# Two 7x7 grouped convolutions: from multiply-adds on VectorE to row-banded matmuls on TensorE

## The chip, the cores and the metric

The kernel runs on one core of a Trainium2 chip. The metric is the device time of one execution in microseconds (us). The core has a matrix engine (TensorE, PE in the profile, with PEld for its weight loads), a vector engine (VectorE, DVE), an activation engine (ScalarE, ACT), GpSimd (POOL) and a queue engine (SyncE, SP). Sixteen DMA engines move data between device memory (DRAM) and the on-chip memory SBUF, whose 128 partitions are the rows of every tile. Matmuls write into PSUM, which has eight banks of 128 partitions x 512 floats.

## The reference, cut to what matters

All numbers are 32-bit floats. x has 2 images of 256 channels, 64 x 64 pixels.

```
# layer 0: global attention over the 4096 pixels, 8 heads of 32 channels, then a 1x1 fuse
attn = softmax(q k^T);  fuse = attn v
x = conv1x1(concat[x, fuse], Wf) * m + x * (1 - m)          # m: mask, resized bilinearly
# layer 1: channel gate, attention in 8x8 windows (4 heads of 64), then the spatial gate:
x = x * sigmoid(mlp(x));  x = x + window_attention(x) @ out_w
x = x.reshape(b, 4, 64, h, w).transpose(0, 2, 1, 3, 4).reshape(b, 256, h, w)   # channel shuffle
y = conv7x7(x, sa_w1, pad 3, groups 64)      # 4 input channels -> 1 output channel, 64 groups
y = relu(bn1(y + sa_b1))
y = conv7x7(y, sa_w2, pad 3, groups 64)      # 1 input channel -> 4 output channels, 64 groups
return x * sigmoid(bn2(y + sa_b2))
```

Group g of the first convolution reads the four channels g, 64 + g, 128 + g and 192 + g of the unshuffled x, and makes one channel; the second makes the four gates of the same group out of it.

## The kernel before, in words

First q, k and v of layer 0 are computed for both images, 16 chunks of 512 pixels, and stored in DRAM. Then one function, `pipeline`, runs everything else in an order written out by hand (`tc.manual_schedule()`): each engine executes its instructions in the order in which the Python code emits them, and waits on semaphores where data are not ready. Two copies of it are built, `arm("a")` and `arm("b")`, with and without a shift of the softmax by a row maximum; a flag computed on the chip picks one. The profile is of arm a.

The main loop goes over 1024 slots (b, c, g, m): image, chunk of 512 query pixels, half of the heads, block of 128 key pixels. A slot has `scores(i + 1)` (four matmuls with 32 rows of weights each, side by side in the array, L398; two exponentials on ScalarE, L406) and `products(i)` (four matmuls for attention times v, L418, and four for the row sums, L421, each 32 columns wide, side by side). The scores use PSUM tiles of two banks, of which there are three (`psum2`); convolutions and stages take theirs from the same three. `load_piece` asks for the k and v of eight slots, two pieces ahead, on SP's queue.

When a chunk's 64 slots are over, `stage(b, c)` does the rest of layer 0 and layer 1's gate and window attention for those 8 image rows. It is a generator: each fourth slot runs it to its next `yield`, 14 steps in all, so that its matmuls stand between those of the slots. Its last step writes the 8 rows into two zero-bordered images in SBUF, `xp[0]` and `xp[1]` (L632), and queues the convolutions whose rows are complete.

The convolutions before are on VectorE. `conv1(b, r0, r1)` makes up to 16 rows: for each of 49 taps and of the two channel halves one instruction, `z = xp[shifted] * w + z` (`tap`, L650 for the first and L652 for the rest), then a matmul with a 0/1 matrix that adds partition halves (`fold`, L669) and a ReLU with the batch norm as scale and bias into `yp` (L670). `conv2` does 49 taps per channel half on `yp`; then tanh and a rescaling on ScalarE make the sigmoid (L433, L434), VectorE multiplies by x (L695), and two stores on GpSimd's queue write the result (L699). `run_convs(2.2)` emits taps of a planned 2.2 us after each slot, so VectorE's other work stands between taps. After the last slot a loop emits what is left: the last stage and the convolutions that remain.

Of the kernel before, what the change touches and what calls it, by code (L numbers as in the profile page):

```python
# [34 lines left out]
HP = H + 2 * PAD  # L35
# [7 lines left out]
def conv_seq_kernel(ctx: ExitStack, tc: tile.TileContext, a, out):  # L43
    nc = tc.nc
    const = ctx.enter_context(tc.tile_pool(name="const", bufs=1))
    dram = ctx.enter_context(tc.tile_pool(name="dram", bufs=1, space=bass.MemoryType.DRAM))
# [17 lines left out]
    def load(name, shape, src, eng, pool=const):  # L64
        t = pool.tile(shape, F32, name=name)
        eng.dma_start(t, src)
        return t

    xp = []
    for kc in range(KC):  # L70
        t = const.tile([P, HP, HP], F32, name=f"xp_{kc}")
        nc.gpsimd.memset(t, 0.0)
        xp.append(t)
    yp = const.tile([P, HP, HP], F32, name="yp")
    nc.gpsimd.memset(yp, 0.0)
# [12 lines left out]
    }  # L88
    k_s, v_s = (
# [119 lines left out]
    sw1 = load("sa_w1", [P, 2, KS * KS], a["sa_w1"], nc.scalar)  # L209
    sw2 = load("sa_w2", [P, 2, KS * KS], a["sa_w2"], nc.scalar)  # L210
# [3 lines left out]
    def batch_norm(name, vec, n):  # L214
        t = const.tile([P, 5, n], F32, name=name)
        if vec.shape[0] == P:
            nc.scalar.dma_start(t, vec)
        else:
            for h in range(2):
                nc.scalar.dma_start(t[64 * h : 64 * h + 64], vec)  # L220
        g, beta, mean, var, cbias = (t[:, i, :] for i in range(5))
        sc = const.tile([P, n], F32, name=name + "_sc")
        sh = const.tile([P, n], F32, name=name + "_sh")
        nc.vector.tensor_scalar_add(sc, var, EPS)
        nc.scalar.activation(sc, sc, AF.Sqrt)
        nc.vector.reciprocal(sc, sc)
        nc.vector.tensor_mul(sc, sc, g)
        nc.vector.tensor_sub(sh, cbias, mean)
        nc.vector.tensor_mul(sh, sh, sc)
        nc.vector.tensor_add(sh, sh, beta)  # L230
        return sc, sh

    sc1, sh1 = batch_norm("bn1", a["bn1"], 1)
    sc2, sh2 = batch_norm("bn2", a["bn2"], 2)

    for t in (sc2, sh2, cb2):
        nc.vector.tensor_scalar_mul(t, t, 0.5)


    fold = const.tile([P, P], F32, name="fold")  # L240
    for i in range(2):
        for j in range(2):
            nc.vector.tensor_copy(
                fold[64 * i : 64 * i + 64, 64 * j : 64 * j + 64],
                ident[64 * i : 64 * i + 64, 64 * i : 64 * i + 64],
            )

# [17 lines left out]
    taps = [(dy, dx) for dy in range(KS) for dx in range(KS)]  # L265


    def conv_rows(b):
        if b + 1 < B:
            steps = {1: (13, 10), 3: (29, 26), 5: (45, 42), 7: (64, 64)}  # L270
        else:
            steps = {1: (13, 10), 3: (29, 26), 5: (45, 42), 6: (53, 50), 7: (64, 64)}
        r1 = r2 = 0
        parts = {}
        for c, (e1, e2) in steps.items():
            parts[c] = (split(r1, e1), split(r2, e2))
            r1, r2 = e1, e2
        return parts

    def split(r0, r1):  # L280
        n = -(-(r1 - r0) // 16)
        cuts = [r0 + (r1 - r0) * i // n for i in range(n + 1)]
        return list(zip(cuts, cuts[1:]))

# [5 lines left out]
    def pipeline(arm, shifted, pools):  # L290
        kvp, qp, ep, fp, xpool, gp, wp, cp = pools
# [139 lines left out]

        def sigmoid(t, z, bias, scale):
            nc.scalar.activation(t, z, AF.Tanh, bias=bias, scale=scale)  # L433
            nc.scalar.activation(t, t, AF.Copy, bias=0.5, scale=0.5)  # L434
# [34 lines left out]
        def stage(b, c):  # L469
# [159 lines left out]
            yield  # L629
            for oc in range(KC):  # L630
                r = PAD + WS * c
                nc.vector.tensor_add(  # L632
                    xp[oc][:, r : r + WS, PAD : PAD + W].rearrange("p r (w c) -> p w r c", c=WS),
                    y[:, oc, :].rearrange("p (w r c) -> p w r c", w=NW, r=WS),
                    u[:, oc, :].rearrange("p (w r c) -> p w r c", w=NW, r=WS),
                )
            if c in parts[b]:
                for r0, r1 in parts[b][c][0]:
                    convs.append(conv1(b, r0, r1))
                for r0, r1 in parts[b][c][1]:  # L640
                    convs.append(conv2(b, r0, r1))

        parts = [conv_rows(b) for b in range(B)]

        def tap(dst, src, wgt, r0, r1, i, first):
            dy, dx = taps[i]
            view = src[:, dy + r0 : dy + r1, dx : dx + W]
            wi = wgt[:, i : i + 1]
            if first:
                nc.vector.tensor_scalar_mul(dst, view, wi)  # L650
            else:
                nc.vector.scalar_tensor_tensor(dst, view, wi, dst, ALU.mult, ALU.add)  # L652
# [3 lines left out]
        def conv1(b, r0, r1):  # L656
            n = r1 - r0
            z = cp.tile([P, 16, W], F32, tag="acc", name=f"acc{arm}_{b}_{r0}")[:, 0:n, :]
            for kc in range(KC):
                for i in range(len(taps)):  # L660
                    tap(z, xp[kc], sw1[:, kc, :], r0, r1, i, kc == 0 and i == 0)
                    yield n * W / 960 + 0.16
            yield 0
            yield 0
            s = psum2(f"fold{arm}_{b}_{r0}")
            sr = s.rearrange("p a (r w) -> p (a r) w", w=W)
            for q0 in range(0, n, 8):
                q1 = min(q0 + 8, n)
                nc.tensor.matmul(sr[:, q0:q1, :], fold, z[:, q0:q1, :], start=True, stop=True)  # L669
            nc.scalar.activation(  # L670
                yp[:, PAD + r0 : PAD + r1, PAD : PAD + W],
                sr[:, 0:n, :],
                AF.Relu,
                bias=sh1,
                scale=sc1,
            )
            yield 0


        dst = [out[b].rearrange("(j k h) r w -> h k j r w", k=2, h=2) for b in range(B)]  # L680

        def conv2(b, r0, r1):
            n = r1 - r0
            for kc in range(KC):
                z = cp.tile([P, 16, W], F32, tag="z", name=f"z{arm}_{b}_{r0}_{kc}", bufs=2)
                z = z[:, 0:n, :]
                for i in range(len(taps)):
                    tap(z, yp, sw2[:, kc, :], r0, r1, i, i == 0)
                    yield n * W / 960 + 0.16

                def gate(z=z, kc=kc):
                    sigmoid(z, z, sh2[:, kc : kc + 1], sc2[:, kc : kc + 1])

                def finish(z=z, kc=kc):
                    nc.vector.tensor_mul(  # L695
                        z, z, xp[kc][:, PAD + r0 : PAD + r1, PAD : PAD + W]
                    )
                    for h in range(2):
                        nc.gpsimd.dma_start(  # L699
                            dst[b][h, kc, :, r0:r1, :], z[64 * h : 64 * h + 64]  # L700
                        )

                at(2, gate)
                at(4, finish)

        def run_convs(budget):
            while convs and budget > 0:
                cost = next(convs[0], None)
                if cost is None:
                    convs.popleft()  # L710
                elif cost == 0:
                    return
                else:
                    budget -= cost
# [21 lines left out]
        for i, (b, c, g, m) in enumerate(slots):  # L736
            now[0] = i
            if m % PB == 0:
                load_piece(i // PB + 2)
            if g == KC - 1 and m == 0:  # L740
                nxt = (b, c + 1) if c + 1 < NCHUNK else (b + 1, 0)
                if nxt[0] < B:
                    load_q(*nxt)
            if i + 1 < len(slots):
                scores(i + 1)
            products(i)
            if g == KC - 1 and m == NMB - 1:
                at(4, lambda b=b, c=c: stages.append(stage(b, c)))
                if c == NCHUNK - 1 and b + 1 < B:
                    at(32, lambda b=b: load_mask(b + 1))  # L750
            run_later()
            if i % 4 == 0:
                run_stages()
            run_convs(2.2)
        while stages or convs or later:
            now[0] += 1
            run_later()
            run_stages()
            run_convs(2.2)

    def arm(name, shifted):
        with (
# [7 lines left out]
            tc.tile_pool(name=f"c{name}", bufs=1) as cp,  # L770
            tc.manual_schedule(),
        ):
            pipeline(name, shifted, (kvp, qp, ep, fp, xpool, gp, wp, cp))
# [71 lines left out]
```

## Time and profile before

| what | value |
|---|---|
| median of 3 runs | 4376.79 us (4374.94 to 4377.25) |
| the profiled execution's own time | 4377.27 us |
| its span, first to last instruction | 4375.5 us |
| mean granted TensorE clock | 0.94 |
| busy TensorE / VectorE / ScalarE | 3830.4 / 2530.2 / 2319.5 us |
| last copy of the last slot's result (L427) | starts at 3884.6 us |
| rows of the last stage written (L632) | starts at 3954.51, takes 1.29 us |
| last store issued (L699) | 4368.50 us |

How to read it: the page shows the busy share of each engine in 40 slices of the span, in tenths, and under PEclk the clock that TensorE was granted. In the group list each row is a line of the code, an engine, an operation and its tiles, how often, the total busy us, the mean ns of one, and the idle time of that engine just before them with what ended it. An fp32 matmul shows as two records. Matmuls that run side by side overlap, so busy time divided by the count is less than the mean of one. The DMA view gives packets, bytes and the share of the 16 DMA engines' time for each queue, and for each group of transfers the median us from issue to landing.

### The profile page before, as it was taken

To read this page: it belongs to the slowest core of one execution; us is meant where nothing else is said; L and a number is where in the kernel's file an instruction comes from. 1 tells how busy PE (TensorE), PEld (TensorE's weight loads), DVE (VectorE), ACT (ScalarE), POOL (GpSimd) and SP (SyncE) were. 2 spreads that over 40 slices of the span, in tenths; PEclk is the share of its full clock that TensorE was granted. 3 is DMA by queue.
4 is the path that set the end of the run, shared out by engine and by line. 5 is a ranking of instruction groups with operands and counts; after the bars stand their busy time and mean duration, and the time that the engine had idled before them with its cause. 6 is when DMAs were issued, how large, how long until landed. Compare 5 with 4: busy or idle time off the path is not lost.

```text
span 4375.5 us, 63766 instructions
## 1 busy us (share of the span) xinstructions
PE 3830.4 (88%) x28080; PEld 1125.9 (26%) x28080; DVE 2530.2 (58%) x2727; ACT 2319.5 (53%) x2503; POOL 39.5 (1%) x65
## 2 busy tenths in 40 slices
PE   9999999999999999999999999999999999970000
PEld 3422222222222222222222222222222232220000
DVE  2200111188306785577636889973177736779998
ACT  2246566656666566656565656566666666540000
POOL 1000000000000000000000000000000000000000
PEclk9999999999999999999999999999999999995555
DMA  4331111111111111111111111111111111000000
GB/s 160 137 97 54 44 44 44 39 39 47 47 44 44 35 49 49 44 41 43 54 44 44 40 44 50 43 47 47 39 44 40 49 49 44 30 6 5 2 3 9
DMA packets 74734, 200.79 MB, mean 46 GB/s; under 512 B 17552, under 2 KB 19152, under 8 KB 74448
## 3 DMA queue, kind: packets, MB, share of 16 engines
q1 hardware_dynamic: 67616, 185.62, 12.4%
q0 software_dynamic: 2432, 8.39, 0.8%
q8 instruction: 222, 3.64, 0.3%
q10 hardware_dynamic: 4400, 2.61, 0.2%
q14 instruction: 64, 0.52, 0.0%
HBM read 163.04 MB, written 33.55 MB: 45 GB/s over the span
## 4 chain that ended last, share of the span: by engine, by line
PE 74%; DVE 15%; ACT 4%; issue 1%; DMA 0%; POOL 0%; DVEq 0%
PE sa L398 24%; PE ava L418 21%; PE dna L421 18%; DVE za L652 7%; DVE acca L652 5%; PE qka L529 3%; PE hya L480 2%; ACT ea L406 2%; DVE rda L429 1%; PE opa L621 1%; PE vwa L546 1%; PE ca1a L503 1%; PE pta L596 1%; PE ca2a L511 1%; PE oa L604 1%
## 5 line engine op out<-in xcount | busy, mean ns | idle before, releaser
L406 ACT ACTIVATE ea<-sa 128x1024 f32<-128x1024 f32 x2048 | 1982.1, 1022 | 967.4 <-PE sa L398 961.8
L398 PE MATMUL sa<-qa,ka 32*128 32x512 f32 x8192 | 1213.9, 644 | 50.0 <-DVE ewa L576 24.3
L418 PE MATMUL ava<-ea,va 128*32 128x512 f32 x8192 | 1101.5, 610 | 4.3
L421 PE MATMUL dna<-ea,ones 128*32 128x512 f32 x8192 | 1075.3, 597 | 0.0
L652 DVE SCALAR_TENSOR_TENSOR acca<-xp,sa_w,acca 128x1024 f32<-128x1024 f32 (+5 forms) x970 | 1039.3, 1071 | 33.1
L652 DVE SCALAR_TENSOR_TENSOR za<-yp,sa_w,za 128x1024 f32<-128x1024 f32 (+4 forms) x960 | 1028.6, 1071 | 32.7
L398 PEld LDWEIGHTS sa<-qa,ka 32*128 32x128 f32 x8192 | 334.2, 184 | 880.7 <-issue 368.1
L429 DVE RECIPROCAL rda<-rda 128x512 f32<-128x512 f32 x32 | 107.3, 3353 | 771.2 <-ACT rda L427 771.2
L421 PEld LDWEIGHTS dna<-ea,ones 128*32 128x32 f32 x8192 | 267.9, 111 | 621.2 <-issue 621.2
L418 PEld LDWEIGHTS ava<-ea,va 128*32 128x32 f32 x8192 | 161.9, 108 | 791.8 <-issue 761.3
L669 PE MATMUL folda<-acca,fold 128*128 128x512 f32 (+4 forms) x38 | 19.1, 627 | 290.7 <-DVE acca L652 290.7
L632 DVE TENSOR_TENSOR xp<-ya,ua 128x512 f32<-128x512 f32 x32 | 21.6, 689 | 434.4 <-ACT ya L628 434.4
L529 PE MATMUL qka<-ua,qkv_w 128*128 128x512 f32 x256 | 128.3, 625 | 28.6 <-ACT qka L537 24.9
L433 ACT ACTIVATE za<-za,bn_sh,bn_sc 128x1024 f32<-128x1024 f32 (+4 forms) x20 | 21.4, 1072 | 230.5 <-DVE za L652 230.5
L521 DVE TENSOR_TENSOR ua<-x1a,sga 128x1024 f32<-128x1024 f32 x16 | 19.6, 1225 | 160.2 <-ACT sga L519 160.2
L670 ACT ACTIVATE yp<-folda,bn_sh,bn_sc 128x1024 f32<-128x1024 f32 (+5 forms) x10 | 10.4, 1045 | 191.6 <-PE folda L669 191.6
L537 ACT ACTIVATE qka<-qka,qkv_b 128x512 f32<-128x512 f32 x64 | 44.0, 687 | 125.6 <-PE qka L529 125.6
L488 DVE SCALAR_TENSOR_TENSOR ta<-hya,bf,mca 128x512 f32<-128x512 f32 x32 | 23.9, 747 | 112.0 <-PE hya L480 112.0
L669 PEld LDWEIGHTS folda<-acca,fold 128*128 128x128 f32 x38 | 7.3, 216 | 305.7 <-issue 301.5
L621 PE MATMUL opa<-ota,out_w 128*128 128x512 f32 x128 | 63.5, 618 | 13.3 <-ACT ya L628 12.4
L529 PEld LDWEIGHTS qka<-ua,qkv_w 128*128 128x128 f32 x256 | 43.9, 191 | 113.3 <-ACT qka L537 52.0
L135 PE MATMUL q<-x,WqT 128*128 128x512 f32 x128 | 61.3, 621 | 5.7 <-DMA WqT<-in_WqT_dram 5.7
(99 smaller groups left out, 1467.2 us busy)
## 6 DMA issues: line engine op xcount, KB each, us to landing
ka<-ks SPq DMA_DIRECT2D x128, 512.0 KB, 3.2
va<-vs SPq DMA_DIRECT2D x128, 512.0 KB, 3.2
x<-in_x_dram SPq DMA_DIRECT2D x16, 512.0 KB, 4.0
ks<-kst SPq DMA_DIRECT2D x32, 256.0 KB, 2.0
qs<-qst SPq DMA_DIRECT2D x16, 512.0 KB, 2.6
vs<-vst SPq DMA_DIRECT2D x32, 256.0 KB, 3.6
qa<-qs SPq DMA_DIRECT2D x16, 512.0 KB, 4.4
xa<-in_x_dram SPq DMA_DIRECT2D x16, 512.0 KB, 3.7
```

Source lines behind the costliest of these rows:

```text
L135: nc.tensor.matmul(s[:, g, :], w[:, kc, g * P : (g + 1) * P], rhs, start=(kc == 0), stop=(kc == KC - 1),)
L398: nc.tensor.matmul(o, k[r, cols], q[r, g, :], start=True, stop=not shifted)
L406: nc.scalar.activation(e[:, 2 * hh : 2 * hh + 2, :], tiles[hh], AF.Exp, scale=SCALE0)
L418: nc.tensor.matmul(acc[0][r, :], v[:, m % PB, r], e[:, j, :], start=start, stop=stop)
L421: nc.tensor.matmul(acc[1][r, :], ones[:, 0:32], e[:, j, :], start=start, stop=stop)
L429: nc.vector.reciprocal(rd, rd)
L480: nc.tensor.matmul(s[:, oc, :], wf[:, kc, oc * P : (oc + 1) * P], xw[kc] if kc < KC else f[:, kc - KC, :], start=(kc == 0), stop=(kc == 2 ...
L503: nc.tensor.matmul(s[0:CR, 0, :], cw1[:, kc, :], x1[:, kc, :], start=(kc == 0), stop=(kc == KC - 1))
L529: nc.tensor.matmul(s[:, j, :], wqkv[:, kc, o : o + P], u[:, kc, :], start=(kc == 0), stop=(kc == KC - 1),)
L537: nc.scalar.activation(qk[:, n, :], s[:, j, :], AF.Identity, bias=bqkv[:, n : n + 1])
L621: nc.tensor.matmul(s[:, oc, :], wo[:, kc, oc * P : (oc + 1) * P], ot[:, kc, :], start=(kc == 0), stop=(kc == KC - 1),)
L652: nc.vector.scalar_tensor_tensor(dst, view, wi, dst, ALU.mult, ALU.add)
```

## The change

Both convolutions become matmuls. A block is a strip of image rows: `BLOCKS = ((0, 0, 25), (16, 25, 39), (33, 39, 64))` are (first row loaded, first row made, end of rows made); each loads `RB = 31` rows. The partitions of a tile hold rows (4 channels x 31 rows, and a partition of ones for the bias), the free dimension holds columns of the image. For each group and each of the 7 horizontal taps a 128 x 32 weight matrix, banded along the rows, does all vertical taps and all four input channels at once, accumulating over the 7 horizontal taps in PSUM. The second convolution uses 32 x 128 matrices in the same way. The batch norms are folded into the weights.

These banded weights are built once, ahead of the loop, by transfers on GpSimd's queue: the convolution weights and norm vectors are loaded (1 + 4 + 16 + 16 transfers), scaled by a few small VectorE and ScalarE operations, written to DRAM, two DRAM arrays of 8 x 128 x 32 x 56 floats are filled with zeros (16 transfers), and 62 transfers scatter rows of 56 floats onto the bands.

A stage now ends with its 8 rows added into a tile `xo` and stored to a DRAM image `x_s[b]` by SP. `convolve(b, blocks)` is a generator that goes over 8 groups u of 8 channel groups: it loads x rows and both weight tiles on SP's queue, does `conv1`, `conv2` and `gate`, and stores the result on GpSimd's queue, 4 transfers per block. The x tiles and the ReLU's tiles are double-buffered (u % 2), the weight tiles have 4 buffers. It has 26 steps; one is taken each fourth slot (i % 4 == 2), and one per turn of the loop after the last slot. Image 0 is convolved in one go (three blocks) when its last chunk's stage is done; of image 1 blocks 0 and 1 are queued when the stage of chunk 5 is done and block 2 after the last. `conv1(b, r0, r1)`, `tap`, `fold`, `xp`, `yp` and the budget of `run_convs` are gone.

```diff
-    xp = []
-    for kc in range(KC):
-        t = const.tile([P, HP, HP], F32, name=f"xp_{kc}")
+    xcs, ycs = [], []
+    for u in range(2):
+        t = const.tile([P, UG, len(BLOCKS), WP], F32, name=f"xc{u}")
...
+    x_s = [dram.tile([C, H, W], F32, name=f"xs_{b}") for b in range(B)]
+    w1_s, w2_s = (dram.tile([NU, P, 32, UW], F32, name=f"w{i}s") for i in (1, 2))
...
+    zero = cwp.tile([P, 32 * UW], F32, name="zero")
+    nc.gpsimd.memset(zero, 0.0)
+    for u in range(NU):
+        for d in (w1_s, w2_s):
+            nc.gpsimd.dma_start(d[u].rearrange("p m f -> p (m f)"), zero)
...
+    for d, m, sr, sq in ((w1_s, r1_s, 4, 1), (w2_s, r2_s, 1, 32)):
+        band = d.rearrange("u p m f -> u (p m) f")
+        for q in range(4):
+            for dy in range(KS):
+                r0, r1 = max(0, dy - PAD), min(RB, RB + dy - PAD)
+                at0 = (sr * (1 + r0) + sq * q) * 32 + 1 + r0 - dy + PAD
+                step = 32 * sr + 1
+                nc.gpsimd.dma_start(
+                    band[:, at0 : at0 + step * (r1 - r0 - 1) + 1 : step, :],
+                    spread(m[KS * q + dy : KS * q + dy + 1], r1 - r0),
+                )
...
             for oc in range(KC):
-                r = PAD + WS * c
                 nc.vector.tensor_add(
-                    xp[oc][:, r : r + WS, PAD : PAD + W].rearrange("p r (w c) -> p w r c", c=WS),
+                    xo[:, oc].rearrange("p r (w c) -> p w r c", c=WS),
...
+                nc.sync.dma_start(
+                    x_s[b][oc * P : (oc + 1) * P, WS * c : WS * c + WS, :], xo[:, oc]
+                )
+            if (b, c) in conv_after:
+                convs.append(convolve(b, conv_after[b, c]))
...
+            def load(u):
+                if u >= NU:
+                    return
+                x = xs[u] = xcs[u % 2]
+                for n, blk in enumerate(blocks):
+                    r = BLOCKS[blk][0]
+                    for q in range(4):
+                        gs = slice(NG * q + UG * u, NG * q + UG * u + UG)
+                        nc.sync.dma_start(
+                            x[4 + q : P : 4, :, n, PAD : PAD + W],
+                            x_s[b][gs, r : r + RB, :].rearrange("g r w -> r g w"),
+                        )
+                for ws, d, i in ((w1s, w1_s, 1), (w2s, w2_s, 2)):
+                    t = wsp.tile([P, 32, UW], F32, tag="w", name=f"w{i}{tag}_{u}")
+                    nc.sync.dma_start(t, d[u])
+                    ws[u] = t
+
+            def conv1(u):
...
+                for q in range(2):
+                    for d in range(KS):
+                        for j in range(4):
+                            nc.tensor.matmul(
+                                s[32 * j : 32 * j + 32, q, 0 : nb * W],
+                                w[:, 4 * q + j, d, :],
+                                x[:, 4 * q + j, 0:nb, d : d + W],
+                                start=(d == 0), stop=(d == KS - 1),
+                            )
+                y = ys[u] = ycs[u % 2]
+                nc.scalar.activation(y[:, :, 0:nb, PAD : PAD + W], s[...], AF.Relu)
+
+            def conv2(u):
...
+                            nc.tensor.matmul(
+                                tiles[j // 2][:, j % 2, q * nb * W : (q + 1) * nb * W],
+                                w[r, q, d], y[r, q, 0:nb, d : d + W],
...
+            def gate(u, z):
+                x = xs.pop(u)
+                nc.vector.tensor_mul(z, z, x[:, :, 0:nb, PAD : PAD + W])
...
+                        nc.gpsimd.dma_start(
+                            dst[i, r0:r1, UG * u : UG * u + UG, :], z[p0 : p1 - 3 : 4, :, n, :]
+                        )
+            load(0)
+            yield
+            conv1(0)
+            yield
+            for u in range(NU):
+                load(u + 1)
+                yield
+                conv1(u + 1)
+                yield
+                z = conv2(u)
+                yield
+                gate(u, z)
...
-            run_convs(2.2)
+            if i % 4 == 2:
+                run_convs()
```

## The prediction

> **What bounds the kernel now.** I read the page's slices first, then its costliest groups, then the chain of the end.
>
> ```profile
> PE 3830.4 (88%) x28080; PEld 1125.9 (26%) x28080; DVE 2530.2 (58%) x2727; ACT 2319.5 (53%) x2503; POOL 39.5 (1%) x65
> PE   9999999999999999999999999999999999970000
> DVE  2200111188306785577636889973177736779998
> PEclk9999999999999999999999999999999999995555
> ...
> L398 PE MATMUL sa<-qa,ka 32*128 32x512 f32 x8192 | 1213.9, 644 | 50.0 <-DVE ewa L576 24.3
> L418 PE MATMUL ava<-ea,va 128*32 128x512 f32 x8192 | 1101.5, 610 | 4.3
> ```
>
> TensorE is full until slice 36; in the last four it is idle, at half clock, and VectorE is full. So there are two regimes: attention slots bound by TensorE up to 3884.5 us (last L427 copy, at which the last slot's matmuls end), and a tail of 491 us to 4375.5. The chain inside the tail, window 4000 to 4376, says whose it is:
>
> ```profile
> by line: DVE za L652 48.7%; DVE acca L652 42.1%; issue 3.0%; PE folda L669 1.3%; DVE za L695 1.2%; DVE za L650 0.6%; ACT yp L670 0.5%; ACT za L433 0.3%; POOL out_dram L699 0.3%; ACT za L434 0.3%; DVE acca L650 0.2%
> ```
>
> The taps of L652 are 91% of it. The timeline of VectorE has one reciprocal (L429) per half chunk; two of them, two apart, span a chunk of 64 slots. The first two rows below lie before the first tap, the others among taps:
>
> ```profile
> 571.02 3.35 DVE L429 RECIPROCAL rda<-rda 128x512 f32<-128x512 f32 x1 [54.40 <-ACT rda L427]
> ...
> 794.88 3.35 DVE L429 RECIPROCAL rda<-rda 128x512 f32<-128x512 f32 x1 [54.42 <-ACT rda L427]
> ...
> 3198.11 3.35 DVE L429 RECIPROCAL rda<-rda 128x512 f32<-128x512 f32 x1 [13.60 <-ACT rda L427]
> ...
> 3429.05 3.35 DVE L429 RECIPROCAL rda<-rda 128x512 f32<-128x512 f32 x1 [13.05 <-ACT rda L427]
> ```
>
> A chunk takes 223.9 us without taps and 230.9 with them. From the end of chunk 0 (452.90) to 3885.22 the 15 chunks average 228.8.
>
> **What goes.** The tail's taps; and in the slots 15 x (228.8 - 223.9) = 74 us of stage work waiting behind taps, folds included. That is all: the other tap time lay beside matmuls.
>
> **Matmuls added.** One group u is 56 matmuls in `conv1` and 56 in `conv2`, two records each as everywhere in this profile, four side by side in 32-wide column or row strips, over 64 columns per block. Per record and column L418 gives 1101.5/8192/512 = 0.26 ns (column strips), L398 0.29 ns (row strips). Three blocks (192 columns): 112 x 192 x 0.55 = 11.9 us per group, 95 for image 0. Two blocks: 7.9 per group. Of image 1's first convolution 18 steps fall into slots (queued at slot 952, a step each fourth slot): six `conv1`, five `conv2`, 44 us. Sum 139. These weights have a stride; no row has that. The dear bound is a record that shares nothing: L596 142 ns at 128 columns against 35, which is rival 3. The cheap bound for short ones:
>
> ```profile
> L565 PE MATMUL sca<-qka 64*64 64x64 f32 x1024 | 18.6, 221 | 0.0
> L604 PE MATMUL oa<-pta,vwa 128*64 128x128 f32 x512 | 32.0, 276 | 0.6 <-ACT pta L597 0.6
> ```
>
> 18 ns a record at 64 columns (L565), 62 at 128 with only two side by side (L604): 4 us per group of one block. `conv2` takes two of the three PSUM pairs, so the next `scores` waits for a tanh; bound 0 to 3 us (three ACT passes of about 1 us), I take 1 x 13 = 13.
>
> **Set-up.** GpSimd gets 121 transfers. At 0.52 us of issue each (L699) that is 63 us; one at a time at 2.9 us to landing, 351. Its next duty, the mask's copies, is first read at 456.96 (L444): hidden either way, and the weights are first loaded after slot 568. VectorE's norms wait for the first 37 of these with the projections' bias adds queued behind: 0 to 20 us, I take 5. Stores of `out` go from 40 to 192, 100 us of issue on an idle queue, and a result buffer has two groups of time.
>
> **The loads, which decide.** `load(u)` puts on SP's queue, per block, four loads of x, each 31 rows x 8 x 64 floats, so 248 packets of 256 B; then two weight loads of 917 KB. `conv1(u)` comes one step later, and TensorE works in order: what x is late, every attention matmul behind waits. The DMA view of 30 to 32 us, where the queue q10 carries mostly 256-B packets, and of the second mask load, 4096 packets of 128 B:
>
> ```profile
> q10 hardware_dynamic: 544, 0.12, 30.7%
> ```
>
> ```profile
> GB/s 0 0 0 234 117 23 187 187 421 374 445 398 398 263 170 218 217 217 217 195 148 138 146 151 148 154 143 146 143 143 145 87 17 0 0 0 0 0 0 0
> DMA packets 4256, 1.05 MB, mean 150 GB/s; under 512 B 4128, under 2 KB 4128, under 8 KB 4256
> ...
> mpa<-in_mask_dram SPq DMA_DIRECT2D x1, 512.0 KB, 6.5
> ```
>
> 30.7% of 16 x 2 us over 544 packets is 18 ns of one DMA engine per packet. 128-B packets at about 145 GB/s over 16 engines are 14 ns; all of q10 (0.2% of 16 x 4375.5 over 4400 packets, 593 B each) is 32. So 14 to 32, and 18 is nearest in size.
>
> How many engines share one load? Every transfer of the kernel before begins with 128, 64 or 32 rows, which sixteen engines share equally. 31 is prime: an equal share exists only on one engine. No row shows an unequal deal. The ends are 16 packets per engine (0.3 us, hidden) and 248 on one: 248 x 18 = 4.5 us. I take one engine, because equal shares are the only deal the trace can be showing.
>
> The Trainium skill, page "DMA: Bandwidth & Descriptors", section "Why a DMA increments its semaphore by 16 and not by 1", speaks against this change: the engine count is the largest number up to 16 that divides the slowest dimension, so 127 partitions go to one engine. By that rule 31 rows have one engine and the sum is the slow one below; by the equal pace of the 128-row loads it would be rival 1's.
>
> **Stalls.** Three blocks: 12 x 4.46 = 53.6 us, then the weights' share on that engine (57 KB at 342/16 GB/s, 2.7) and landing (2.0, as ks): 58. The load can start when `gate(u-2)` has freed the buffer, about five slots before `conv1`: 5 x 2.93 plus 4 of stage work = 18 lead. Stall 40, and after it the clock is halved for a while, as after this gap of 3.7 us (timeline):
>
> ```profile
> 3916.67 3.61 PE L529 MATMUL qka<-ua,qkv_w 128*128 128x512 f32 x4 [3.74 <-DVE ua L521]
> ...
> 3925.54 1.98 PE L529 MATMUL qka<-ua,qkv_w 128*128 128x512 f32 x4 [0.78 <-ACT qka L537]
> ```
>
> 3.61 against 1.98: 1.8 us more. So 42 x 8 = 336 in image 0. Two blocks: 35.7 + 4.7 - 18 + 1.8 = 24, x 6 = 145. The next k and v stand behind these loads on SP's queue; they are due 16 slots, 47 us, after they are asked for, and TensorE's own stall covers their delay, so I add nothing; without that cover it would cost up to 54 - 47 = 7 us a group.
>
> **Tail.** `conv1(6)` waits 28, runs 3.8; `conv2(5)` 4.2; ACT and multiply 4; load 40.4; `conv1(7)` 3.8: 84 before the last stage's first matmul, since it is emitted behind them. The stage took 71 (3884.5 to 3955.7), 12 of it behind taps; 59 plus 3 for `conv2` = 62. Store of x 2.6. Then block 2 alone, where each load waits for the gate of two groups before and that for `conv1` of the next: a closed ring of load 17.9 + 4.7, `conv1` 4 and `conv2` 6 (half clock), ACT and multiply 3 = 35.6, x 8 = 285, plus 5 for the last stores.
>
> **Sum.** 3884.5 - 74 + 139 + 13 + 5 = 3967.5; stalls 481; 84 + 62 + 2.6 + 290: 4887 span. The profiled execution was 4377.27 for a span of 4375.5 (1.8 around it) against a median of 4376.79: 4889, so 4890, 12% slower. In packet price t the same sum is about 4033 + 47.6 t: 4700 at 14 ns, 5556 at 32; even at 7.2.
>
> **Rival 1, on the other side: the loads are dealt over all engines.** Then twelve take 12 x 0.42 issue + 2 + weights 3.2 = 10 us, under the lead of 18: no stall. Before the stage 24; the ring is 1.7 issue + 2 + 2.7 + 4 + 6 + 3 = 19.4, x 8 + 5 = 160. 3967.5 + 24 + 62 + 2.6 + 160 + 1.8 = 4218, 3.6% faster. It decides as soon as a load costs less than 7.2 ns x 248 = 1.8 us. For it: all loads shown are spread. Against: none shown has an indivisible row count.
>
> **Rival 2: one engine, dearer packets.** Rows of x lie 16 KB apart, the 256-B rows priced here lie together. At 32 ns, 5556.
>
> **Rival 3: dealt, but strided weights make TensorE the cost.** At unshared prices (142/128 ns per record and column) image 0 adds 12 x 8 = 96, image 1 4 x 11 half groups = 44, the ring perhaps 30: 4388, level with before. For it: unseen stride. Against: L565 and L604 reach their peaks at 64 and 128 columns.
>
> **How the numbers follow.** About 0.2% is what a measurement can tell from no change. One engine 0.77, of which 0.10 lies above 5300 (rival 2); rival 1 0.16, since dealing equally is all that the rows show but nothing excludes the other; rival 3 0.07, split 0.03, 0.02, 0.02. Faster 0.19, same 0.02, slower 0.79. The likeliest case alone spans 4700 to 5300. To hold 8 in 10 over both signs I reach down to rival 1 at 4210 and up to 26.6 ns, 5300; left out are the dear packets, 0.10, and rival 1's lower half, 0.08.
>
> **What would show it.** Idle time of TensorE before `conv1`'s matmuls, released by DMA of the x buffer, about 40 us at three blocks, 22 at two; landing of the last x load of a group near 50, 36 and 18 us; slices of PE in image 1's first half falling below 9 with a DMA share near 1; a tail of some 440 us whose chain is DMA. If instead x lands within 5 us and PE idles little, the dealing was misjudged; if landings are long but PE does not wait, the lead was.

## The result, and the profile after

The changed kernel takes 4718.43 us (median of 4 runs, 4716.7 to 4723.51) against 4377.02 before (4374.94 to 4377.4): a ratio of 1.0783, 95% interval 1.0764 to 1.0802. The profiled execution took 4723.51 us, with a span of 4721.7 and a mean granted clock of 0.929.

The page of the changed kernel, engine totals, slices and groups:

```profile
PE 4098.8 (87%) x33418; PEld 1394.8 (30%) x33418; DVE 462.4 (10%) x775; ACT 2330.8 (49%) x2549; POOL 220.5 (5%) x344
PE   9999999999999999999575768999999997985533
DVE  2200101010110110101001000110101010010100
PEclk9999999999999999999787888999999998987755
...
L755 PE MATMUL c1a<-xc,w1a 128*32 128x192 f32 (+2 forms) x2688 | 126.4, 375 | 529.0 <-DMA w1a<-w1s 503.0
...
L776 PE MATMUL c2a<-yc,w2a 32*128 32x192 f32 (+2 forms) x2688 | 171.1, 415 | 0.0
```

VectorE has gone from 2530.2 to 462.4 us, and TensorE, which was full until slice 36, now has holes: slices 20 to 25, when image 0 is convolved, slice 34, when image 1's first convolution runs, and the last five. 529 us of its idle time stand directly before the matmuls of `conv1` (L755). The timeline of TensorE in image 0's groups shows the wait of each in brackets:

```profile
2276.29 7.17 PE L755 MATMUL c1a<-xc,w1a 128*32 128x192 f32 x112 [30.19 <-DMA w1a<-w1s]
...
2335.44 6.62 PE L755 MATMUL c1a<-xc,w1a 128*32 128x192 f32 x112 [28.38 <-DMA w1a<-w1s]
...
2423.37 7.02 PE L755 MATMUL c1a<-xc,w1a 128*32 128x192 f32 x112 [26.65 <-DMA w1a<-w1s]
```

The releaser named is the weight load w1a, not x. That is the order on SP's queue: w1a is issued behind the twelve loads of x and lands last, so the bracket carries their time. The loads of x themselves, by tile (issue in ns: least, median, most), and the DMA view of 2226 to 2270 us, in which only one group's loads run after the first four slices:

```profile
L738 SPq DMA_DIRECT2D xc<-xs x192: 628/3592/7452, 2226.2 to 4683.3; - x192
```

```profile
DMA  8893001000000000000000000000000000000000
GB/s 130 294 397 122 18 18 33 18 17 17 17 17 17 17 17 17 17 18 18 17 18 17 17 18 18 17 18 17 18 17 17 17 17 17 17 17 17 17 17 17
```

One load has 248 packets of 256 B, so 3592 ns is 14.5 ns per packet, or 17.7 GB/s. The view shows just this pace, 17 to 18 GB/s, at a busy share that rounds to zero tenths of the sixteen engines (0.08 from 2236 to 2266 us): about one engine works.

VectorE's reciprocals (L508 now), two apart, span a chunk of 64 slots without convolutions; the third line is the last one of the slots:

```profile
2943.08 3.35 DVE L508 RECIPROCAL rda<-rda 128x512 f32<-128x512 f32 x1 [56.88 <-ACT rda L506]
...
3166.92 3.35 DVE L508 RECIPROCAL rda<-rda 128x512 f32<-128x512 f32 x1 [54.40 <-ACT rda L506]
...
4312.19 3.35 DVE L508 RECIPROCAL rda<-rda 128x512 f32<-128x512 f32 x1 [11.78 <-ACT rda L506]
```

That is 223.84 us, the 223.9 of before; the ten chunks without convolutions take 223.8 to 225.5. Yet the slots end at about 4311.5, 427 us later than before, and the tail after them takes 410 us where it took 491. The chain of the tail's ring, window 4450 to 4722:

```profile
by line: SPq L738 35.9%; PE c2a L776 20.9%; DMA w1a<-w1s 20.4%; PE c1a L755 8.2%; issue 1.9%; DVE za L798 1.8%; ACT za L792 1.6%; ACT za L786 1.6%; SPq L744 1.5%; PE opa L696 1.5%; POOL out_dram L803 0.9%; PE oa L679 0.8%; DMA xs<-xoa 0.8%;
```

56% of it is the issue of x's loads and the landing of w1a; VectorE, which owned 91% of the old tail's chain in its taps, has 2%.

### The profile page after: what moved, and what is told of

The parts are those of the page before. It is cut to its first block, busy times and chain, and to the rows that moved or that the text cites. A ratio compares the mean times of both kernels' runs of the same rounds, so it can differ in the third digit from the quotient of the medians.

```text
span 4721.7 us, 73526 instructions
## 1 busy us (share of the span) xinstructions
PE 4098.8 (87%) x33418; PEld 1394.8 (30%) x33418; DVE 462.4 (10%) x775; ACT 2330.8 (49%) x2549; POOL 220.5 (5%) x344
## 4 chain that ended last, share of the span: by engine, by line
PE 69%; SPq 14%; DMA 4%; ACT 4%; DVE 3%; issue 1%; POOL 0%; DVEq 0%; ACTq 0%
PE sa L477 20%; PE ava L497 18%; PE dna L500 16%; SPq L738 13%; PE c2a L776 4%; DMA w1a<-w1s 4%; PE c1a L755 3%; PE qka L604 2%; PE hya L555 2%; ACT ea L485 1%; PE opa L696 1%; PE vwa L621 1%; DVE rda L508 1%; PE pta L671 1%; PE oa L679 1%
## 5 line engine op out<-in xcount | busy, mean ns | idle before, releaser
L755 PE MATMUL c1a<-xc,w1a 128*32 128x192 f32 (+2 forms) x2688 | 126.4, 375 | 529.0 <-DMA w1a<-w1s 503.0
L755 PEld LDWEIGHTS c1a<-xc,w1a 128*32 128x32 f32 x2688 | 108.6, 165 | 556.1 <-issue 544.3
L508 DVE RECIPROCAL rda<-rda 128x512 f32<-128x512 f32 x32 | 107.3, 3353 | 1503.8 <-ACT rda L506 1503.8
L803 POOL DMA_DIRECT2D out_dram<-za x192 | 132.6, 698 | 2468.2 <-DVE za L798 2361.5
L776 PE MATMUL c2a<-yc,w2a 32*128 32x192 f32 (+2 forms) x2688 | 171.1, 415 | 0.0
L776 PEld LDWEIGHTS c2a<-yc,w2a 32*128 32x128 f32 x2688 | 166.1, 336 | 13.9 <-issue 9.2
L786 ACT ACTIVATE za<-c2a 128x768 f32<-128x768 f32 (+2 forms) x48 | 26.1, 594 | 172.2 <-PE c2a L776 172.1
L707 DVE TENSOR_TENSOR xoa<-ya,ua 128x512 f32<-128x512 f32 x32 | 21.7, 692 | 857.5 <-PE opa L696 857.5
L798 DVE TENSOR_TENSOR za<-za,xc 128x1536 f32<-128x1536 f32 (+2 forms) x24 | 29.4, 1226 | 711.2 <-ACT za L792 711.1
```

The costliest lines, as they stand in the source:

```text
L508: nc.vector.reciprocal(rd, rd)
L755: nc.tensor.matmul(s[32 * j : 32 * j + 32, q, 0 : nb * W], w[:, 4 * q + j, d, :], x[:, 4 * q + j, 0:nb, d : d + W], start=(d == 0), stop=( ...
L776: nc.tensor.matmul(tiles[j // 2][:, j % 2, q * nb * W : (q + 1) * nb * W], w[r, q, d], y[r, q, 0:nb, d : d + W], start=(d == 0), stop=(d = ...
L803: nc.gpsimd.dma_start(dst[i, r0:r1, UG * u : UG * u + UG, :], z[p0 : p1 - 3 : 4, :, n, :])
```

## The experiments

The theory: 31 rows go to one DMA engine, the loads therefore last 3.6 us each, and TensorE, which works in order, stands before `conv1`. The rivals: the number of packets or SP's issue is too dear whatever the rows, or the matmuls with strided weights are the cost.

**rows30: 30 rows per load instead of 31.** The bands of the weights stay, so what the 31st row contributes is missing from the sums.

```
-  x[4 + q : P : 4, ...],              x_s[b][gs, r : r + RB, :]
+  x[4 + q : 4 * 30 + q + 1 : 4, ...], x_s[b][gs, r : r + 30, :]
```

> Each x load takes 30 rows instead of 31; the 31st row of every block stays zero, so the last row's contribution to the convolutions is left out. Theory (equal shares only): 30 rows are shared by 15 engines, 16 packets each, a load costs its issue of about 0.4 us instead of 3.6; TensorE's 529 us of waiting before conv1 shrink to the ring of the tail (some 7 us a group), total about 4265 us (4200 to 4330). Rival A (256-byte packets are slow to issue or to move, whoever carries them): 30/31 of the packets, so the load takes 3.5 us, total about 4695. Rival B (only row counts that 16 divides are spread): 30 stays on one engine, also about 4695.

Measured: 4257.56 us (one execution, as in rows29 and split_contig), with 4376.11 for the kernel before on the same chip. The loads by tile, the group of `conv1`, and the pace of all transfers in 2226 to 2270 us, the same window as above:

```profile
L738 SPq DMA_DIRECT2D xc<-xs x192: 822/823/1647, 2228.4 to 4221.8; - x192
```

```profile
L755 PE MATMUL c1a<-xc,w1a 128*32 128x192 f32 (+2 forms) x2688 | 91.6, 307 | 103.2 <-DMA w1a<-w1s 90.4 <-DMA xc<-xs 11.6 <-issue 1.2
```

```profile
GB/s 11 30 112 318 400 249 68 89 82 63 32 75 66 102 241 430 417 424 111 48 309 134 0 0 0 0 0 101 340 160 105 64 58 96 77 58 63 134 352 430
```

A load has 240 packets instead of 248, and the kernel takes 461 us less: an issue lasts 0.82 us, there is no stall of note in the slots (they end at 3983), and 103 us of waiting are left, nearly all in the tail. In slices 7 to 12 of the window SP issues loads of x alone, and they move at 32 to 89 GB/s, two to five times the pace of 31 rows: more than one engine carries them. Both rivals are out: rival A, since nearly as many packets of the same size were fast, and rival B, since 16 does not divide 30.

**rows29: 29 rows, a prime again.** The same edit with 29; two rows' contributions are missing.

> Each x load takes 29 rows; two rows of every block stay zero and their contribution is left out. 29 is prime like 31. Theory (equal shares only): still one engine, 232 packets at 14.6 ns, 3.4 us a load, total 4718 - 0.065 x 695 = 4673 us, slower than the 30-row kernel by some 400 although it moves less. Rival A: the same 4673, but then it must be faster than the 30-row kernel. A rival by which any change of the count breaks the pattern: fast like the 30-row kernel.

Measured: 4676.19 us. The load by tile:

```profile
L738 SPq DMA_DIRECT2D xc<-xs x192: 628/3357/6787, 2227.3 to 4636.3; - x192
```

3357/3592 is 0.935, as 29/31 is: the same 14.5 ns per packet. The smaller load is four times as long as that of 30 rows, and the kernel 419 us slower. So neither packets nor bytes decide, but what divides the row count. This is the rule of the Trainium skill, page "DMA: Bandwidth & Descriptors", section "Why a DMA increments its semaphore by 16 and not by 1": the largest number up to 16 that divides the slowest dimension. 31 and 29 have 1, 30 has 15, and the three runs order themselves by it; that it is just 15 engines for 30 rows, no run shows.

**split: all 31 rows, as loads of 16 and 15.** Nothing is left out.

```
-  nc.sync.dma_start(x[4 + q : P : 4, ...], x_s[b][gs, r : r + RB, :]...)
+  for k0, k1 in ((0, 16), (16, RB)):
+      nc.sync.dma_start(x[4 * (1 + k0) + q : 4 * k1 + q + 1 : 4, ...],
+                        x_s[b][gs, r + k0 : r + k1, :]...)
```

> The same 31 rows in two loads, of 16 and of 15 rows; nothing left out. Theory: 16 and 15 engines, 8 packets each per load, 24 loads at 0.35 to 0.45 us of issue per group of three blocks = 10 us, plus 5 for the first weights, under the lead of 18; no wait before conv1 in the slots; the tail's ring about 3.5 + 5 + 3.2 + 7.1 + 2.5 = 21 us a group instead of 32.6. Total about 4275 us, faster than the kernel before by 2 to 3%. Rival A (packets cost the same wherever they go): as many packets, about 4720. Rival C (the weights' 1.8 MB per group are what TensorE waits for, as the releaser's name w1a says): unchanged, about 4700.

Measured: 4322.81 us (4320.08 to 4325.6), ratio to before 0.9879, interval 0.9862 to 0.9895. Loads and `conv1`:

```profile
L739 SPq DMA_DIRECT2D xc<-xs x384: 557/844/1807, 2226.3 to 4287.5; - x192
```

```profile
PE c1a L756 <- DMA w1a<-w1s: 135.7, 12, 20.6
PE c1a L756 <- issue: 14.6, 3, 6.3
```

That is 1.2% faster than before where I expected 2 to 3: the direction held, the size fell short by 48 us. I had priced the issue of a short load like that of a 128-row load; it takes 0.84 us, as much as one of 30 rows, and three blocks now have 24: 20 us of issue, about as long as the lead that `load` has over `conv1` (15 to 28 us in the changed kernel). Some waits in the slots stay (the slots end at 4018, 35 us later than with 30 rows) and the tail's ring takes 23.6 us instead of 21.6. Rival A is out, with as many packets as in the changed kernel, and so is rival C, with the same weights.

**split_contig: split, and both matmuls read their weights as consecutive floats.** The values read are then not those of the convolution; sizes and counts are.

```
-  w[:, 4 * q + j, d, :]   # conv1
+  w[:, 32 * (KS * (4 * q + j) + d) : 32 * (KS * (4 * q + j) + d) + 32]
-  w[r, q, d]              # conv2
+  w[r, P * (KS * q + d) : P * (KS * q + d) + P]
```

> The two-load kernel, in which the weights of each matmul are read as consecutive floats instead of with a step of 56 (conv1) or 14 (conv2) floats; they are then not the convolution's weights, so the convolutions' values are left out and only their time is kept. Theory (the stride halves the weight load): conv2's 112 records fall from 7.09 us to about 4.2, as their weight loads fall from 336 ns to the 183 of the scores', conv1's 64-column group from 3.2 to about 2.1 and the 192-column one from 7.1 to 5.6; total about 80 to 100 us under the two-load kernel. Rival (128 columns for 64 to 192 columns of data are bound by the load however they lie): conv2 stays at 7.1, no change of the total.

Measured: 4244.18 us, 79 less than split. The weight loads (PEld) of `conv2`, of split and then of split_contig:

```profile
L777 PEld LDWEIGHTS c2a<-yc,w2a 32*128 32x128 f32 x2688 | 166.1, 336 | 14.0 <-issue 9.6 <-PE ava L497 4.2 <-ACT za L787 0.2
```

```profile
L777 PEld LDWEIGHTS c2a<-yc,w2a 32*128 32x128 f32 x2688 | 91.8, 193 | 14.2 <-issue 9.6 <-PE ava L497 4.2 <-ACT za L787 0.4
```

With a step of 14 floats between weights a load takes 336 ns instead of 193, and `conv2` is bound by it: 57.2, 56.8 and 57.2 us for 896 records at 192, 128 and 64 columns, 7.09 us per group whatever the width. Read consecutively they take 38.9, 27.3 and 30.7: 74 of the 79 us, so the rival that the step does not matter is out. `conv1`, whose loads have 32 columns instead of 128, does not gain what I expected of it: its matmuls take 106.1 us in all against 103.5 in split.

**rb30: the whole convolution in blocks of 30 rows.**

```
-RB = 31
-BLOCKS = ((0, 0, 25), (16, 25, 39), (33, 39, 64))
+RB = 30
+BLOCKS = ((0, 0, 24), (17, 24, 40), (34, 40, 64))
```

Where 31 or 32 stood for RB in the bands and the load, RB stands.

> The whole convolution with strips of 30 loaded rows (blocks 0 to 24, 24 to 40, 40 to 64), nothing left out. Theory: as many transfers, packets per engine and matmuls as the 30-row kernel that left a row out, so its 4257.6 us again, 2.7% faster than the kernel before. Rival (the missing row made that kernel fast, not the sharing): back towards 4700.

Measured: 4252.21 us (4248.29 to 4255.68), ratio 0.9714, interval 0.9698 to 0.973. The convolution is whole, with one row less per load than in the changed kernel: 466 us less. The rival that the missing row made rows30 fast is out.

**deep: rb30 with a third x tile, and `load(u + 2)` issued behind `conv2(u)`.**

```
-                x = xs[u] = xcs[u % 2]
+                x = xs[u] = xcs[u % 3]
...
+            load(1)                 # behind load(0)
...
-                load(u + 1)
...
+                load(u + 2)         # behind z = conv2(u)
```

> The 30-row strips, a third x buffer, and each group's loads asked for two groups ahead, right behind conv2. Theory (in the tail's ring a load waits for the gate two groups before, 21.7 us a group): the ring opens, TensorE's 3.2 + 7.1 = 10.3 us a group bound it, 8 x 11.4 = 91 us less, and some 20 us of waits before conv1 at two blocks go: 4147 us. Rival (the transfers bound the tail: 1.9 MB a group at 342 GB/s, 5.6 us, and SP's issue of 4 x 0.82 + 0.9 one after the other): 10 us a group as well or slightly more, so 4150 to 4170; rival (x lands late because SP's queue holds it behind the weights of the group before, which wait for conv2): about 16 us a group, 4195.

Measured: 4172.83 us (4172.48 to 4173.97), ratio 0.9534, interval 0.9518 to 0.955. The timeline of TensorE, of rb30 and then of deep: the last `conv1` of two blocks, which stands ahead of the last stage, and the tail's ring:

```profile
4010.17 4.88 PE L755 MATMUL c1a<-xc,w1a 128*32 128x128 f32 x112 [15.93 <-DMA w1a<-w1s]
...
4119.04 3.22 PE L755 MATMUL c1a<-xc,w1a 128*32 128x64 f32 x112 [10.59 <-DMA w1a<-w1s]
4122.19 7.09 PE L776 MATMUL c2a<-yc,w2a 32*128 32x64 f32 x112
4139.78 3.22 PE L755 MATMUL c1a<-xc,w1a 128*32 128x64 f32 x112 [10.51 <-DMA w1a<-w1s]
```

```profile
3991.09 3.31 PE L757 MATMUL c1a<-xc,w1a 128*32 128x128 f32 x112
...
4089.34 3.22 PE L757 MATMUL c1a<-xc,w1a 128*32 128x64 f32 x112
4092.49 7.09 PE L778 MATMUL c2a<-yc,w2a 32*128 32x64 f32 x112
4100.90 3.22 PE L757 MATMUL c1a<-xc,w1a 128*32 128x64 f32 x112 [1.31 <-DMA w1a<-w1s]
```

The ring goes from 20.8 to some 10.8 us per group: load and matmuls now run beside each other. By the stages of the two profiles, block 2 alone, from its first load to the end, takes 61 us less (107.0 for 168.2), and the stretch from the end of the slots to the last stage's first matmul 19 less (13.2 for 32.6), most of it the wait of 15.93 us. The slots themselves end at 3981.1 instead of 3982.4, because rb30 had hardly a stall there to lose. So the 20 us of waits at two blocks came as expected, and the 91 of the ring were too many: its turns are 10 us shorter, not 11.4, and the first group or two gain little. That is why the time comes out 26 us above 4147, near the 4150 to 4170 of the first rival; but after the first two turns TensorE waits 1.31 us for w1a at most, so its matmuls, not the transfers, fill most of a turn.

**deep_contig: deep, and VectorE puts each group's second weights into consecutive order.** To make room for the copy, the tile of zeros is cut to a quarter and each zero transfer into four.

```
+            def straighten(u):
+                t = wsp.tile([P, 2 * KS, P], F32, tag="v", name=f"v{tag}_{u}", bufs=1)
+                nc.vector.tensor_copy(t, w2s[u].rearrange("p m (i f) -> p f (m i)", i=4))
+                w2s[u] = t
...
-                                w[r, q, d],
+                                w[r, KS * q + d, :],
```

> The kernel before it in this list, and VectorE copies each group's second weights into consecutive order (128 x 1792 floats, about 2 us, 24 times); nothing left out. Theory (conv2 is bound by weight loads with a step, 57 us for eight groups at any width): conv2 falls to the 39, 27 and 31 us of the run with consecutive weights at three, two and one block, of which the tail keeps what its loads of about 8 us a group allow: 18 + 30 + 8 x 2 = 64 less, 4085 us. Rival (the copies stand in VectorE's queue ahead of the stages' work and give it back, 24 x 2 = 48 us): 4130.

Measured: 4125.14 us (4122.1 to 4130.92), ratio 0.9425, interval 0.9409 to 0.9441: the fastest version, 5.7% faster than the kernel before. Its groups:

```profile
L776 DVE COPY va<-w2a 128x1792 f32<-128x1792 f32 x24 | 42.0, 1752 | 12.4 <-DMA w2a<-w2s 12.4
```

```profile
L760 PE MATMUL c1a<-xc,w1a 128*32 128x192 f32 (+2 forms) x2688 | 88.7, 297 | 28.6 <-DMA w1a<-w1s 28.4 <-issue 0.2
```

The 24 copies take 42 us of VectorE. `conv2` falls to 38.9, 28.9 and 39.0 us at three, two and one block, where deep had 57.2, 56.8 and 57.2. The slots end at 3942.1 instead of 3981.1, so the gain there arrives in full and the copies hold nothing up. The tail gains only 6 us, and block 2 alone next to nothing (106.3 us for 107.0). There `conv1` waits 28.6 us in all, where deep waited 18.4, and `conv2` waits 7.9, 5.5 of them on the copies: together the 18 us that the shorter `conv2` would have saved. With shorter matmuls the transfers are late next. That makes it 40 us above the 4085 that I expected. The time is near the rival's 4130, but not by its cause, since the slots gave nothing back.

## Why the prediction was right, point by point

The forecast was 12% slower by one mechanism; it is 7.8% slower by that one. Along the prediction's own terms:

| term | predicted us | measured us |
|---|---|---|
| slots of attention alone, 3884.5 - 74 | 3810.5 | 3822 (15 chunks at 224.7, the mean of the ten without convolutions) |
| set-up | 5 | 0 (first scores at 256.8, before 257.5) |
| matmuls in slots, at full clock | 139 | 150 (from deep: 58 `conv1`, 93 `conv2`) |
| PSUM pairs | 13 | 9 (rest of deep's slots) |
| stalls before `conv1` in slots | 454 | 294 (228 at three blocks, 66 at two) |
| halved clock after them | 27 | 36 (rest) |
| end of slots | 4448.5 | 4311.5 |
| to the last stage's first matmul | 84 | 80 |
| the stage and its store | 64.6 | 69 |
| block 2 alone, to the end | 290 | 261 |

The 74 us for waits behind taps were somewhat too many: the two chunks that the prediction read took 223.9 us, others without convolutions take up to 225.5.

**One engine: right**, shown by rows30 and rows29 and not only by the trace. **The price per packet was the mis-sized term**: 18 ns from the first mask loads, 14.5 in fact, near the cheap end of 14 that the 128-B packets gave. With it the prediction's formula, 4033 + 47.6 t, says 4723; the profiled execution took 4723.5. So near a hit has luck in it, as the other terms show: the first loads of a group are issued sooner than 14.5 ns a packet (the four of the ring take 12.3 us), w1a lands some 8 us behind the start of its issue instead of 4.7, and the lead in image 0 was some 22 us instead of 18.

**Stalls: place and shape right**, 22 to 36 us at three blocks for 40 and 7 to 15 at two for 22. Twelve loads take 42 us instead of 53.6, and this and the longer lead, less the later landing of w1a, are the 160 us missing. The lower clock is there: from 2226 to 2880 us the granted clock was 0.82, and 1.00 in rows30, and `conv1` at three blocks takes 57.0 us for 896 records behind stalls and 38.1 in deep without them. (The prediction's pair of rows differs by 1.6 us, not by the 1.8 that it took; with 14 stalls that is under 3 us.)

**Matmuls: the sum nearly right, its parts not.** `conv1` cost less than I took (4.8 us per group of three blocks, for half of 11.9), `conv2` more (7.15 at three blocks for half of 11.9, 7.09 at two for half of 7.9 and in the ring for 6). That is the part of rival 3 that is real: the strided weights bind `conv2`, and in split they cost 79 us. They weigh little in the verdict beside the stalls, but with the loads dealt they are what lies between deep, 4.7% faster than before, and deep_contig, 5.7%.

Rival 3 itself was added up too low. Its own price, 142 ns for 35, is four times the shared one, so image 0 would add three times 95 us and not 96, and image 1's slots three times 44; that comes to about 4665 and not 4388. At that size its total would have been hard to tell from one engine's. What rules it out as the cause is rows30, which has the same matmuls with the same weights and is 461 us faster.

**Tail: right in its making.** The turn of the closed ring that is shown took 32.8 us for 35.6 (the mean is 32.6): loads 12.4 for 17.9, w1a 8.1 for 4.7, `conv1` and `conv2` 10.2 for 10, the rest 2.1 for 3. The rows of TensorE and of SP's queue in it:

```profile
4564.96 3.22 PE L755 MATMUL c1a<-xc,w1a 128*32 128x64 f32 x112 [22.57 <-DMA w1a<-w1s]
4568.11 7.09 PE L776 MATMUL c2a<-yc,w2a 32*128 32x64 f32 x112
4597.39 3.22 PE L755 MATMUL c1a<-xc,w1a 128*32 128x64 f32 x112 [22.18 <-DMA w1a<-w1s]
```

```profile
4544.49 12.26 SPq L738 DMA_DIRECT2D xc<-xs  x4
4556.85 3.53 SPq L744 DMA_DIRECT2D w1a<-w1s  x1
...
4577.31 11.97 SPq L738 DMA_DIRECT2D xc<-xs  x4
```

**Rival 1 was the right picture of the kernel with the loads dealt.** It said 4218; rows30 measured 4257.6 and the whole convolution in blocks of 30 rows 4252.2. Of the 34 us between it and rb30, 15 lie in the slots (3982.4 for 3967.5), 9 between them and the last stage (32.6 for 24, with the wait of 15.93 us), 3 in the stage and its store, and 8 in block 2 alone (168.2 for 160).

## What to carry to other kernels

Look at the first dimension of every transfer before its bytes: here the issue of 31 rows held the queue for 3.6 us and that of 30 rows for 0.8, and one row turned a kernel 2.9% faster than before into one 7.8% slower. A long wait is named after the transfer that lands last, so read the queue in front of it. Where an in-order engine meets such a load, what counts is the load's length against its lead: a third buffer and an earlier request gave 79 us, after the loads had been made short.

## What the runs showed of the hardware

- Loads of 31 and of 29 rows moved their 256-B packets at 14.5 ns each (17.7 GB/s), with a busy share of 0.08 of the sixteen engines at 31 rows, and SP's queue was held by the issue of such a load as long as that took (3.59 us), and by w1a's issue behind them too (3.53 us, against 0.56 with 30 rows, both medians). Whether the queue waits for the engine or the engine for the queue, no run separates; the shortest issue of such a load, 0.63 us, speaks for the first.
- Loads of 30 rows and of 16 or 15 rows all took 0.82 to 0.84 us of issue, so halving a load doubled the queue's time.
- The step between weights costs TensorE time: 336 ns against 193 for 32 x 128, but 154 against 142 for 128 x 32, where the matmuls got no faster.
- The ring in the tail ran at a granted clock of 0.54 (4459 to 4721 in the changed kernel, 4122 to 4255 in rows30), and `conv2` took 7.09 us per group there as in the slots at full clock, again bound by its weight loads. Idle gaps alone do not explain the clock: in deep, where TensorE's records fill 95% of 4089 to 4150 us, the granted clock was 0.56.
